# Time attention in blocks of 64 keys, one sequence per half of the rows, on 64x32 tiles

## The chip, the cores and the metric

The kernel runs on one core of a Trainium2 chip. Every array is fp32. The metric is the device time of one execution in microseconds; the lower, the better. PE is TensorE (matmuls; PEld its weight loads), DVE VectorE, ACT ScalarE, POOL GpSimd, SP the engine that issues most DMAs.

## The reference

The input x has the shape 2 x 256 x 128 x 128: batch, time T, band F, channel C. Three residual steps follow each other. Time attention runs causally over the 256 times of each of the 2 x 128 (batch, band) pairs, band attention over the 128 bands within a distance of 16, and the feed-forward step has 512 hidden channels. The change concerns the first.

```python
xt = _ln(x, ln_t_w, ln_t_b).transpose(0, 2, 1, 3)
x = x + _mha(xt, t_wi, t_bi, t_wo, t_bo, 4, causal).transpose(0, 2, 1, 3)
x = x + _mha(_ln(x, ln_f_w, ln_f_b), f_wi, f_bi, f_wo, f_bo, 4, band)
x = x + gelu(_ln(x, ln_n_w, ln_n_b) @ w1.T + b1) @ w2.T + b2

def _mha(x, wi, bi, wo, bo, h, mask):        # dh = 32
    q, k, v = split_heads(x @ wi.T + bi)
    attn = softmax(q k^T / sqrt(dh) + mask)
    return (attn @ v) @ wo.T + bo
```

## The kernel before

The work is cut into groups of 512 tokens, on which every step works with tiles of 128 partitions by 512 columns. The first 128 groups (class OverTime) are time attention; each holds two whole sequences of 256 times, s = 0 and 1. After them come 128 groups of band attention (OverBands) and 128 of feed-forward (FeedForward), in runs of 8 and 8. Nothing reorders the instructions: each engine executes in the order in which `run` writes them, a loop over n that does one part of several groups in each turn (software pipelining). The order of the matmuls of the scores is a table written by hand, TIME_ORDER.

One group of time attention goes through these steps, spread over several turns:

- statistics, root, normalize, turn, fetch: layer norm on DVE (roots of four groups at once by ACT's Ln and Exp, sharpened on DVE by `refine`), transposed by DVE and through a DRAM tile on SP's queue into xnT, channels on partitions.
- queries_keys, take_query, take_key: two products of 512 columns into PSUM banks, copied by ACT into qT and kT. `product` makes each as four matmuls on 128x32 tiles of PE (rows x columns of the array), which write 32 partitions each.
- values, take_values: four blocks of 128 tokens, tokens on partitions, into two banks (vp0, vp1), copied by ACT into v.
- scores: keys on partitions, queries on columns, by 32x64 tiles. The first 128 keys of a sequence meet all its queries (first_scores, into the four banks a0 to a3, one for each head); the second 128 keys meet only the second 128 queries (second_scores, banks b0 to b3) one turn later. Keys are taken in halves of 64, so that columns ahead of a half are skipped.
- first_weights, second_weights: ACT's Exp into p0 and p1, head by head. mask_first, mask_second: POOL zeroes what lies above the diagonal (affine select). add: POOL adds p1 to the second half of p0, for the sums.
- weigh: PE sums the weights over the keys by a product with ones (into rp) and weighs the values (into op), on 128x32 tiles.
- invert (ACT: Ln, Exp of -Ln) and divide (DVE: a Newton step, u, then oT = op times u); output (PE, into yp), finish (DVE adds the residual) and store.

A turn n does the second part of the scores of group n (`old`), the first part of n + 1 (`new`), the queries, keys and values of n + 2, weigh of n - 1 and output of n - 2. Eight PSUM banks carry the roles a0 to a3 and b0 to b3; hand_banks_on moves the roles round after every turn, and Attention.place says which step borrows which bank. A bank is free for the next writer when its last reader is done, and PE executes in order, so a matmul that waits for a bank holds up all that is behind it. A fp32 matmul shows as two records in the trace.

All instructions bear the line of a helper (L907 before, `InOrder`), so groups are told apart by the names of their tiles.

Of the kernel before, what the change touches and what calls it, by code (L numbers as in the profile page):

```python
# [33 lines left out]
HALF = P // 2  # L34
LARGE = 1e20
# [334 lines left out]
class Group:  # L370
# [50 lines left out]
    def root_in_spare(self):  # L421
        path = self.path
        self.root_by_scalar(path.ps[path.banks["b2"]][:, BANK - self.mv.shape[1] :])

    def root_in_bank(self):
        path = self.path
        self.root_by_scalar(path.ps[path.banks["b2"]][:, 0 : self.mv.shape[1]])
# [84 lines left out]
    def queries_keys(self):  # L512
        pass
# [47 lines left out]
class Attention(Group):  # L561
    which = None
    swapped = ()
# [7 lines left out]
    def queries_keys(self):  # L571
        path = self.path
        wf = path.k.wf[self.which]
        self.qp = path.bank([P, NT * P], "qp", self.place.get("qp", path.held.pop("qp", None)))
        product(path, self.qp, wf[:, 0:P], self.xnT)

        self.kp = path.bank([P, NT * P], "kp", self.place.get("kp"))
        product(path, self.kp, wf[:, P : 2 * P], self.xnT)
# [11 lines left out]
    def values(self):  # L590
        path = self.path
        wv = path.k.wf[self.which][:, 2 * P : 3 * P]
        self.vp = path.bank([P, NT, P], "vp", self.place.get("vp"))
        for i in range(NT):
            product(path, self.vp[:, i], self.xnT[:, i * P : (i + 1) * P], wv, turn=2 if i in self.swapped else 0)
# [19 lines left out]
    def divide(self):  # L615
# [10 lines left out]
        vector.scalar_tensor_tensor(u, self.rp, 2.0, self.r0, ALU.subtract, ALU.mult)  # L626
        self.oT = path.work.tile([P, NT * P], F32, name="oT", bufs=2)
        vector.tensor_tensor(by_rows(self.oT), by_tile(self.op), by_tile(u), ALU.mult)

    def output(self):  # L630
        path = self.path
        self.yp = path.bank([P, NT, P], "yp", self.place.get("yp", path.held.pop("yp", None)))
        for i in range(NT):
            product(path, self.yp[:, i], self.oT[:, i * P : (i + 1) * P], path.k.wn[self.which])
# [11 lines left out]
def product(path, out, weights, x, start=True, stop=True, turn=0):  # L646


    for c in range(P // D):
        path.tensor.matmul(out[rows_of(c)], weights[:, rows_of((c + turn) % NT)], x, start=start, stop=stop)  # L650


class OverTime(Attention):
# [4 lines left out]
    swapped = (1, 3)  # L658
    early, late = (1, 2), (0, 3)

    def values(self):
        path = self.path
        wv = path.k.wf[self.which][:, 2 * P : 3 * P]
        self.vp = [path.bank([P, 2, P], "vp", self.place.get(f"vp{s}")) for s in range(2)]
        for i in range(NT):
            product(
                path, self.vp[i // 2][:, i % 2], self.xnT[:, i * P : (i + 1) * P], wv, turn=2 if i in self.swapped else 0
            )
# [7 lines left out]
    def first_tiles(self):  # L676
        path = self.path

        self.p0 = path.work.tile([P, 2, H, 2 * P], F32, name="p0", tag="p", bufs=3)
        self.s0 = {h: path.bank([P, 2, 2 * P], "sp", path.banks[f"a{h}"]) for h in range(H)}  # L680

    def second_tiles(self):
        path = self.path

        self.p1 = path.work.tile([P, 2, H, 2, P], F32, name="p1", tag="h", bufs=2)
        self.s1 = {h: path.bank([P, 2, P], "sp", path.banks[f"b{h}"]) for h in range(H)}

    def first_scores(self, h, s, e):
        r, a = rows_of(h), 2 * s * P
        self.path.tensor.matmul(  # L690
            self.s0[h][e : e + HALF, s, e:], self.kT[r, a + e : a + e + HALF], self.qT[r, a + e : a + 2 * P],
            start=True, stop=True,
        )

    def second_scores(self, h, s, e):
        r, a, q = rows_of(h), (2 * s + 1) * P, P - HALF - e
        self.path.tensor.matmul(
            self.s1[h][e : e + HALF, s, q:], self.kT[r, a + q : a + q + HALF], self.qT[r, a + q : a + P],
            start=True, stop=True,
        )  # L700

    def first_weights(self, heads):
        for h in heads:
            self.path.scalar.activation(self.p0[:, :, h], self.s0[h], AF.Exp)

    def second_weights(self, heads):
        for h in heads:
            self.path.scalar.activation(self.p1[:, :, h, 0], self.s1[h], AF.Exp)

    def mask(self, blk, base=0):  # L710
        path = self.path
        path.gpsimd.affine_select(
            out=blk, in_=blk, compare_op=ALU.is_ge, fill=path.zero, base=base,
            pattern=[[0, 2], [0, H], [1, blk.shape[-1]]], channel_multiplier=-1,
        )

    def mask_first(self):
        self.mask(self.p0[:, :, :, 0:P])

    def mask_second(self):  # L720
        self.mask(self.p1[0:HALF, :, :, 0], -HALF)
        self.mask(self.p1[HALF:P, :, :, 0, 0:HALF])

    def add(self, s):
        self.path.gpsimd.tensor_tensor(self.p1[:, s, :, 1], self.p1[:, s, :, 0], self.p0[:, s, :, P : 2 * P], ALU.add)

    def weigh(self):
        path, v = self.path, self.v
        rp = path.bank([P, 2, 2, P], "rp", self.place.get("rp"))
        for n in range(2):  # L730
            for h in range(H):
                w = self.p1[:, :, h, 1] if n else self.p0[:, :, h, 0:P]
                path.tensor.matmul(rp[rows_of(h), :, n], path.k.ones[:, 0:D], w, start=True, stop=True)
        op = path.bank([P, 2, 2 * P], "op", self.place.get("op"))
        for s in range(2):
            for h in range(H):
                r = rows_of(h)
                path.tensor.matmul(op[r, s, :], v[:, 2 * s, r], self.p0[:, s, h], start=True, stop=False)
# [774 lines left out]
```

## Time and profile before

| | before |
|---|---|
| median of 3 runs (lowest, highest) | 2633.42 us (2632.39, 2633.75) |
| span of the profiled execution | 2631.9 us |
| PE busy, share of the span | 99% |
| DVE, ACT, POOL busy | 81%, 70%, 74% |
| DMA queue of the loads and stores, share of 16 engines | 50.5% |
| granted PE clock | 1.000 |

The page gives the profiled execution by its span, from its first to its last instruction; no other time of that execution is given. Rows of a timeline give start, length, engine and operation, out<-in by the names of the tiles, the number of instructions merged into the row, and in brackets the idle time before it and what ended it. `128*32 128x512` is a PE tile of 128 rows by 32 columns with 512 columns of moving data. Rows of groups give, behind the count, the busy time, the mean length of one in ns and the idle time before.

### The profile page before, as it was taken

Reading aid. Unit: us, or ns where it says so; the run is one execution under the profiler, and the core shown is the slowest. Engines: PE = TensorE matmul, PEld = TensorE weight load, DVE = VectorE, ACT = ScalarE, POOL = GpSimd, SP = SyncE. Lnnn points to the kernel's source line nnn. Section 1 sums busy time; section 2 is a strip of 40 time slices with the busy share of each in tenths; the row PEclk is TensorE's granted clock in tenths of the full one; section 3 lists DMA queues with packets and bytes.
Section 4 is the critical chain, followed back from the end, with each engine's and each line's share of the span. In section 5 each row is a group of like instructions: output and inputs, shape, how many; then the busy total and the mean of one; then the engine's idle time right before and its main releaser. Section 6 shows DMA issues by size and latency. Waiting matters only on the chain.

```text
span 2631.9 us, 156460 instructions
## 1 busy us (share of the span) xinstructions
PE 2617.8 (99%) x68688; PEld 1837.4 (70%) x68688; DVE 2140.8 (81%) x6410; ACT 1838.8 (70%) x3543; POOL 1958.6 (74%) x2311
## 2 busy tenths in 40 slices
PE   9999999999999999999999999999999999999999
PEld 6666666666766767666777776667676677777776
DVE  8888888888888887977878779788797797887974
ACT  7989988999899875564655746647557466475573
POOL 7999999999999987666667666665776666757762
PEclk9999999999999999999999999999999999999999
DMA  6656555565565454445454544554454445554543
GB/s 155 167 149 158 149 149 149 155 155 149 149 158 149 122 127 119 115 123 127 118 124 124 123 122 117 126 128 120 122 126 120 120 119 131 123 120 123 123 104 88
DMA packets 469797, 344.97 MB, mean 131 GB/s; under 512 B 43120, under 2 KB 404464, under 8 KB 469104
## 3 DMA queue, kind: packets, MB, share of 16 engines
q1 hardware_dynamic: 468408, 334.41, 50.5%
q8 instruction: 540, 8.85, 1.5%
q14 instruction: 153, 1.25, 0.2%
q10 hardware_dynamic: 696, 0.46, 0.1%
HBM read 167.98 MB, written 166.72 MB: 127 GB/s over the span
## 4 chain that ended last, share of the span: by engine, by line
PE 99%; DVE 0%; issue 0%; DMA 0%; ACT 0%; ACTq 0%; DVEq 0%
PE bank L907 99%; DMA x<-in_x 0%; DVE xh L907 0%; DVE bank L907 0%; DVE res L907 0%; DVE stats L907 0%; DVE oT L907 0%; DVE u L907 0%; DVE xnT L907 0%; ACTq L907 0%; ACT p L907 0%; DVE vy L907 0%; ACT lnv L907 0%; DVE mv L907 0%; ACT root L907 0%
## 5 line engine op out<-in xcount | busy, mean ns | idle before, releaser
L907 ACT ACTIVATE hT<-bank,b 128x512 f32<-128x512 f32 x512 | 348.1, 688 | 524.2 <-PE bank L907 483.2
L907 POOL TENSOR_SCALAR_AFFINE_SELECT pf<-pf 128x512 f32<-128x512 f32 x768 | 477.7, 637 | 185.3 <-ACT pf L907 159.1
L907 PEld LDWEIGHTS bank<-w2T_sb,hT 128*32 128x32 f32 x16384 | 467.4, 110 | 54.8 <-issue 29.0
L907 PE MATMUL bank<-xnT,wf 128*32 128x512 f32 x4096 | 492.4, 592 | 0.5 <-DVE xnT L907 0.5
L907 PE MATMUL bank<-xnT,w1f 128*32 128x512 f32 x4096 | 486.3, 592 | 0.2 <-issue 0.2
L907 PE MATMUL bank<-w2T_sb,hT 128*32 128x128 f32 x16384 | 482.8, 273 | 1.0 <-issue 1.0
L907 ACT ACTIVATE p<-bank 128x512 f32<-128x512 f32 (+1 forms) x1024 | 430.6, 494 | 62.9 <-PE bank L907 62.9
L907 DVE TENSOR_SCALAR xh<-x,mv,rstd 128x160 f32<-128x160 f32 (+1 forms) x1012 | 394.3, 432 | 59.7 <-POOL rstd L907 49.4
L907 POOL TENSOR_SCALAR_AFFINE_SELECT p<-p 128x1024 f32<-128x1024 f32 (+2 forms) x384 | 364.5, 949 | 57.5 <-ACT p L907 49.1
L907 PEld LDWEIGHTS bank<-wf,xnT 128*32 128x32 f32 x8192 | 243.3, 110 | 144.1 <-issue 101.6
L907 POOL TENSOR_TENSOR p<-p,p 128x512 f32<-128x512 f32 x256 | 324.6, 1291 | 10.6
L907 DVE BATCH_NORM_STATS2 stats<-x 128x6 f32<-128x128 f32 x1536 | 329.0, 276 | 3.4 <-DMA x<-in_x 3.4
L907 POOL TENSOR_SCALAR rstd<-mv 128x4 f32<-128x4 f32 x251 | 57.8, 230 | 361.7 <-DVE mv L907 360.5
L907 PEld LDWEIGHTS bank<-xnT,w1f 128*32 128x32 f32 x4096 | 183.6, 110 | 171.6 <-issue 109.6
L907 PE MATMUL bank<-qT,kT 32*64 32x80 f32 (+4 forms) x16384 | 302.0, 271 | 0.1
L907 PEld LDWEIGHTS bank<-qT,kT 32*64 32x64 f32 x16384 | 260.0, 131 | 51.2 <-ACT kT L907 50.6
L907 DVE TENSOR_TENSOR res<-bank,res 128x512 f32<-128x512 f32 (+1 forms) x259 | 170.3, 658 | 153.3 <-PE bank L907 144.7
L907 ACT ACTIVATE pf<-bank 128x512 f32<-128x512 f32 x512 | 265.8, 602 | 35.5 <-PE bank L907 31.3
L907 PE MATMUL bank<-wn,oT 128*32 128x128 f32 x8192 | 283.8, 274 | 0.1
L907 DVE STREAM_TRANSPOSE z<-xh 128x512 f32<-128x512 f32 x380 | 270.3, 711 | 13.3
L907 PE MATMUL bank<-wf,xnT 128*32 128x128 f32 x8192 | 276.5, 273 | 0.0
L907 POOL TENSOR_TENSOR rstd<-rstd,mhalf 128x4 f32<-128x4 f32 x251 | 260.8, 1039 | 20.9
(100 smaller groups left out, 3820.3 us busy)
## 6 DMA issues: line engine op xcount, KB each, us to landing
turned<-z SPq DMA_DIRECT2D x1520, 64.0 KB, 2.7
xnT<-turned SPq DMA_DIRECT2D x380, 256.0 KB, 3.2
x<-res SPq DMA_DIRECT2D x256, 128.0 KB, 2.5
x<-x SPq DMA_DIRECT2D x128, 256.0 KB, 4.1
out<-res SPq DMA_DIRECT2D x252, 128.0 KB, 2.3
x<-in_x SPq DMA_DIRECT2D x124, 256.0 KB, 4.3
x<-in_x SPq DMA_DIRECT2D x4, 128.0 KB, 2.8
x<-in_x SPq DMA_DIRECT2D x6, 64.0 KB, 2.9
```

The source lines that it names most:

```text
L907: return self.tc.keep_in_program_order(emit(*args, **kwargs))
```

## The change

Each of the two sequences of a group now keeps to one half of the partitions, from the values on. Keys go in four blocks b of 64, of which each meets the queries from its own first one on: 256, 192, 128 and 64 columns.

- Values are written by 128x64 tiles, a block of sequence 0 into partitions 0 to 63 and of sequence 1 into 64 to 127.
- Scores keep their 32x64 tiles and their columns. A bank of heads a0 to a3 now holds blocks 0 and 1 (448 of 512 columns), b0 to b3 blocks 2 and 3 (192 columns); the partition half is the sequence.
- Exponentials cover 448 and 192 columns for 512 and 256. Masks are four affine selects of 64 partitions by 512; POOL adds 512, 256 and again 256 columns for the sums.
- Sums and weighted values run on 64x32 tiles: eight matmuls at a time, four heads by two sequences. [...]
- Queries, keys and output of time attention use 128x64 tiles for 128x32.
- The bank roles no longer move; places are fixed (yp in b3, queries and keys in b0, vp0 in a3, vp1 in a0). The roots go into a0, and refine runs within divide.
- The queries of n + 2 move between the scores and weigh; keys, output and values stay behind weigh. The order of Exp changes with it (heads 0, 1, 2 of b, heads 1, 2 of a; late: head 3 of b, heads 3, 0 of a).

On PE, one turn before, from the end of the scores to the start of the next (bank and pair numbers are PSUM banks; wf with xnT are queries and keys where the column count is 512 and values where it is 128; wn with oT is the output):

```order
L907 MATMUL bank_115<-qT,kT 64x64
L907 MATMUL bank_113<-wn_236,oT 32x128 x16
L907 MATMUL bank_112<-p_5261,ones 32x2x128 x4
L907 MATMUL bank_112<-p_5428,ones 32x2x128 x4
L907 MATMUL bank_110<-p_5261,v 32x256 x4
L907 MATMUL bank_110<-p_5428,v 32x128 x4
L907 MATMUL bank_110<-p_5261,v 32x256 x4
L907 MATMUL bank_110<-p_5428,v 32x128 x4
L907 MATMUL bank_109<-xnT,wf_151 32x512 x4
L907 MATMUL bank_111<-xnT,wf_151 32x512 x4
L907 MATMUL bank_113<-wf_151,xnT 32x128 x8
L907 MATMUL bank_115<-wf_151,xnT 32x128 x8
```

and after (pair_123 is b1 and b2, pair_124 a1 and a2, bank_116 b0, bank_117 b3, bank_118 a0, bank_119 a3):

```order
L925 MATMUL bank_117<-qT,kT 64x64 x2
L925 MATMUL bank_116<-xnT,wf_152 64x512 x2
L925 MATMUL pair_123<-p_5657,ones 32x128 x8
L925 MATMUL pair_123<-p_5838,ones 32x128 x8
L925 MATMUL pair_123<-p_5657,ones 32x128 x8
L925 MATMUL pair_124<-p_5657,v 32x256 x8
L925 MATMUL pair_124<-p_5657,v 32x192 x8
L925 MATMUL pair_124<-p_5838,v 32x128 x8
L925 MATMUL pair_124<-p_5838,v 32x64 x8
L925 MATMUL bank_116<-xnT,wf_152 64x512 x2
L925 MATMUL bank_117<-wn_225,oT 64x128 x8
```

The output moved behind the keys, the queries stand alone ahead of the sums, and the instructions of sums and weighted values went from 24 to 56.

Where a turn ends on PE, after: the last rows are the values, then the first scores of the next turn:

```order
L925 MATMUL bank_119<-wf_152,xnT 64x128 x4
L925 MATMUL bank_118<-wf_152,xnT 64x128 x4
L925 MATMUL bank_119<-qT,kT 64x256 x2
L925 MATMUL bank_116<-qT,kT 64x128 x2
L925 MATMUL pair_123<-qT,kT 64x128 x4
```

The values' two banks are again written by the scores: bank_119 by the very next matmul, which waits for ACT's copy of it (v<-bank_119). Before, the first scores wrote other banks than the values did.

On ACT, one turn after, from the copy of the keys on (before, ln and r stood between the six first Exp and the last two, and the query's copy right ahead of the key's):

```order
L925 COPY kT<-bank_116 128x512
L925 COPY v<-bank_119 128x256
L925 COPY v<-bank_118 128x256
L925 ACTIVATE p_8585<-bank_116 128x192
L925 ACTIVATE p_8585<-pair_123 128x192 x2
L925 ACTIVATE p_8584<-pair_124 128x448 x2
L925 ACTIVATE qT<-bank_116,bq_188 128x512
L925 ACTIVATE ln<-pair_123 128x512
L925 ACTIVATE r_8700<-ln 128x512
L925 ACTIVATE p_8585<-bank_117 128x192
L925 ACTIVATE p_8584<-bank_119 128x448
L925 ACTIVATE p_8584<-bank_118 128x448
```

The diff, cut to its core:

```diff
+FIRST = 4 * P - HALF
+SECOND = P + HALF
...
-def product(path, out, weights, x, start=True, stop=True, turn=0):
-    for c in range(P // D):
-        path.tensor.matmul(out[rows_of(c)], weights[:, rows_of((c + turn) % NT)], x, start=start, stop=stop)
+def product(path, out, weights, x, columns=D, start=True, stop=True):
+    for c in range(0, P, columns):
+        path.tensor.matmul(out[c : c + columns], weights[:, c : c + columns], x, start=start, stop=stop)
...
+        for b in range(NT):
+            for s in range(2):
+                a = 2 * s * P + b * HALF
+                path.tensor.matmul(
+                    self.vp[b // 2][half(s), b % 2], self.xnT[:, a : a + HALF], wv, start=True, stop=True
+                )
...
+    def block(self, b):
+        return (0, 2 * P, 0, P)[b], 2 * P - b * HALF
+    def scores(self, b, h, s):
+        sp, r = (self.s1 if b // 2 else self.s0)[h], rows_of(h)
+        a, n = self.block(b)
+        t = 2 * s * P + b * HALF
         self.path.tensor.matmul(
+            sp[half(s), a : a + n], self.kT[r, t : t + HALF], self.qT[r, t : t + n], start=True, stop=True
         )
...
+    def mask(self, p, n):
+        for s in range(2):
+            blk = p[half(s)].rearrange("p h (b q) -> p (h b) q", q=n)[:, :, 0:HALF]
...
+    def add(self):
+        add = self.path.gpsimd.tensor_tensor
+        late = self.folded[:, :, HALF:P]
+        add(self.folded, self.p0[:, :, P : 2 * P], self.p1[:, :, 0:P], ALU.add)
+        add(self.spare, self.p0[:, :, FIRST - HALF : FIRST], self.p1[:, :, P:SECOND], ALU.add)
+        add(late, late, self.spare, ALU.add)
...
+        self.rp, self.op = path.wide
+        tiles = [(h, s) for s in range(2) for h in range(H)]
+        for p, a, at in ((self.p0, 0, 0), (self.folded, 0, P), (self.p0, 2 * P, HALF)):
+            for h, s in tiles:
+                q = 2 * s * P + at
                 path.tensor.matmul(
+                    self.rp[rows_of(h), q : q + P], path.k.ones[half(s), 0:D], p[half(s), h, a : a + P],
+                    start=at == 0, stop=at == HALF,
                 )
...
 TIME_ORDER = """
-    s310 s301 s011 s000 s300 s010 s001 f110 f201 f200 f111 f301 f101 f310 f000 f211
+    030 031 200 201 210 211 220 221 300 301 310 311 320 321 010 011 020 021
...
-        self.banks = dict(zip(("a1", "a2", "b0", "b3", "a0", "a3", "b1", "b2"), range(8)))
+        self.banks = dict(zip(("b0", "b3", "b1", "b2", "a1", "a2", "a0", "a3"), range(8)))
...
-                Attention.place = dict(yp=b["b0"], rp=b["b3"], op=b["a1"], qp=b["a2"], kp=b["b1"], vp0=b["b0"], vp1=b["b2"])
+                Attention.place = dict(yp=b["b3"], qp=b["b0"], kp=b["b0"], vp0=b["a3"], vp1=b["a0"])
...
+            if old is not None and n + 2 >= TURNED:
+                do_at(n + 2, OverTime, "queries", "take_query")
...
             do(n - 1, "weigh")
...
+            if old is not None:
+                old.second_weights((3,))
+                old.mask_second()
+                old.add()
             if new is not None:
                 new.first_weights(new.late)
+            roots = sets[n // 2] if n in (3, 5) else fours.get(n + 2 * NT)
+            if roots is not None:
+                roots.root_in_spare("a0")
...
+                do_at(n + 2, OverTime, "keys", "take_key")
+                do(n - 2, "output")
+            if roots is not None:
+                groups[n - 1].divide(roots.refine)
+            else:
+                do(n - 1, "divide")
```

In TIME_ORDER a row of three digits is block, head, sequence.

More of the change, by code (lines that the diff above doesn't have):

```diff
@@ L510, in second_mask, with queries, keys @@
         pass
-    def queries_keys(self):
+    def queries(self):
+        pass
+    def keys(self):
         pass
@@ L562 @@
     which = None
-    swapped = ()
+    columns = D
     place = {}
@@ L569, in bias, with queries, keys @@
         )
-    def queries_keys(self):
+    def queries(self):
         path = self.path
-        wf = path.k.wf[self.which]
         self.qp = path.bank([P, NT * P], "qp", self.place.get("qp", path.held.pop("qp", None)))
-        product(path, self.qp, wf[:, 0:P], self.xnT)
+        product(path, self.qp, path.k.wf[self.which][:, 0:P], self.xnT, self.columns)
+    def keys(self):
+        path = self.path
         self.kp = path.bank([P, NT * P], "kp", self.place.get("kp"))
-        product(path, self.kp, wf[:, P : 2 * P], self.xnT)
+        product(path, self.kp, path.k.wf[self.which][:, P : 2 * P], self.xnT, self.columns)
     def take_query(self):
@@ L633, in output @@
         for i in range(NT):
-            product(path, self.yp[:, i], self.oT[:, i * P : (i + 1) * P], path.k.wn[self.which])
+            product(path, self.yp[:, i], self.oT[:, i * P : (i + 1) * P], path.k.wn[self.which], self.columns)
     def finish(self):
@@ L663, in values @@
         wv = path.k.wf[self.which][:, 2 * P : 3 * P]
[L664 to L668, printed above, removed]
+        self.vp = [path.bank([P, 2, P], "vp", self.place.get(f"vp{i}")) for i in range(2)]
+        for b in range(NT):
[4 more added lines that the diff above has]
+                )
     def take_values(self):
@@ L748 @@
+        for b in range(NT):
+            p = (self.p0, self.p1)[b // 2]
+            a, n = self.block(b)
+            for h, s in tiles:
+                r, q = rows_of(h), 2 * s * P + b * HALF
+                path.tensor.matmul(
+                    self.op[r, q : q + n], v[half(s), b, r], p[half(s), h, a : a + n], start=b == 0, stop=b == NT - 1
+                )
 TIME_ORDER = """
-    s310 s301 s011 s000 s300 s010 s001 f110 f201 f200 f111 f301 f101 f310 f000 f211
-    f210 f100 f001 s111 f010 s311 s201 f300 f311 s211 f011 s100 s210 s101 s110 s200
+    030 031 200 201 210 211 220 221 300 301 310 311 320 321 010 011 020 021
@@ L751 @@
+    000 001 130 131 110 111 120 121 100 101 230 231 330 331
 """.split()
@@ L760, in time_scores @@
         old.second_tiles()
-    for kind, h, s, e in TIME_ORDER:
-        if kind == "s" and old is not None:
-            old.second_scores(int(h), int(s), int(e) * HALF)
-        if kind == "f" and new is not None:
-            new.first_scores(int(h), int(s), int(e) * HALF)
+    for order in TIME_ORDER:
+        b, h, s = map(int, order)
+        group = old if b // 2 else new
+        if group is not None:
+            group.scores(b, h, s)
 class OverBands(Attention):
@@ L941, in __init__, with single_banks, split_pairs @@
             )
+    def single_banks(self, ctx, name, banks):
+        pool = ctx.enter_context(self.tc.tile_pool(name=name, bufs=1, space=PSUM))
+        for i in banks:
+            self.ps[i] = pool.tile([P, BANK], F32, name=f"bank{i}", tag=f"bank{i}")
+    def split_pairs(self):
+        self.pairs.close()
+        self.single_banks(self.pairs, "rest", range(2, 6))
+        self.rotation = [0, 1, 6, 7, 2, 3, 4, 5]
+        self.next_bank = 0
     def turn_of_bank(self):
-        i, self.next_bank = self.next_bank, (self.next_bank + 1) % 8
+        i = self.rotation[self.next_bank]
+        self.next_bank = (self.next_bank + 1) % len(self.rotation)
         return i
@@ L1227, in start @@
         self.fold_value(0)
-        Attention.place = dict(qp=2, kp=3, vp0=6, vp1=7)
-        first.queries_keys()
+        Attention.place = dict(qp=b["b0"], kp=b["b3"], vp0=b["b1"], vp1=b["b2"])
+        first.queries()
+        first.keys()
         first.take_query()
@@ L1258, in start @@
         first.mask_first()
-        second.queries_keys()
+        second.queries()
+        second.keys()
         second.take_query()
```

166 lines of the change are left out of this document (66 added, 100 removed).

## The prediction

> **What bounds the kernel now.** I read the page first, then busy time by stage, then the timeline of one group in the middle of the time stage, and last the groups of each engine there.
>
> ```profile
> span 2631.9 us, 156460 instructions
> PE 2617.8 (99%) x68688; PEld 1837.4 (70%) x68688; DVE 2140.8 (81%) x6410; ACT 1838.8 (70%) x3543; POOL 1958.6 (74%) x2311
> PE 99%; DVE 0%; issue 0%; DMA 0%; ACT 0%; ACTq 0%; DVEq 0%
> ...
> 24.00:914.00 890.00, 888.17 (x24056) 616.38 (x24048) 755.89 (x2257) 800.47 (x1821) 822.70 (x753) 1.00 0.59 151
> 914.00:2632.00 1718.00, 1708.68 (x44354) 1207.15 (x44354) 1368.05 (x4069) 1024.75 (x1694) 1122.93 (x1535) 1.00 0.48 120
> ```
>
> TensorE (PE) is the bound: it is busy all the span at the full clock and carries the chain that ended last. The change touches the time stage, some 900 us. There POOL is busy 92% and ACT 90%, so they have little room. One group on PE:
>
> ```profile
> 500.68 1.06 PE L907 MATMUL bank<-wf,xnT 128*32 128x128 f32 x32
> 501.67 1.39 PE L907 MATMUL bank<-qT,kT 32*64 32x64 f32 x64
> 502.98 1.08 PE L907 MATMUL bank<-wn,oT 128*32 128x128 f32 x32
> 503.88 1.05 PE L907 MATMUL bank<-p,ones 128*32 128x256 f32 x16
> 504.74 1.48 PE L907 MATMUL bank<-p,v 128*32 128x256 f32 x32
> 506.04 1.90 PE L907 MATMUL bank<-xnT,wf 128*32 128x512 f32 x16
> 507.76 0.95 PE L907 MATMUL bank<-wf,xnT 128*32 128x128 f32 x28
> ...
> 1101.05 3.62 PE L907 MATMUL bank<-xnT,w1f 128*32 128x512 f32 x32
> 1104.48 3.68 PE L907 MATMUL bank<-w2T_sb,hT 128*32 128x128 f32 x128
> 1107.98 3.62 PE L907 MATMUL bank<-xnT,w1f 128*32 128x512 f32 x32
> ```
>
> From start to start a group lasts 507.76 - 500.68 = 7.08 us. An fp32 product shows twice in the trace, so it is two passes. Four tiles run side by side: 32 records of 512 columns are eight passes in 3.43 us, 0.429 each; 128 records of 128 columns are 32 passes in 3.50, 0.109 each; sums, four passes of 256 columns, take 0.86, 0.215 each. The group then reads: values 0.99 (eight passes are 0.87, and 0.11 more before the tile shape changes), scores 1.31 (1.20 and 0.11 for the change back), output 0.90, sums 0.86, weighted values 1.30 (four passes of 256 columns and four of 128), queries and keys 1.72. Each change of tile shape costs about 0.11 us, and there are two per group.
>
> **The change, part by part.** *Sums and weighted values on 64x32 tiles.* Eight tiles instead of four, with keys in blocks of 64. Sums go from four passes of 256 columns to three products of 128, six passes: 6 x 0.109 = 0.65, against 0.86. Weighted values go to passes of 256, 192, 128 and 64 columns, two each: 2 x (0.215 + 0.162 + 0.109 + 0.055) = 1.08, plus 0.03 because eight tiles start staggered, against 1.30. This saves 0.40 if eight tiles of this shape run side by side. No row has 64x32; the nearest has eight tiles too:
>
> ```profile
> 958.18 0.97 PE L907 MATMUL bank<-qT,kT 32*64 32x80 f32 x64
> ...
> L907 PE MATMUL bank<-qT,kT 32*64 32x80 f32 x8192 | 124.0, 240 | 0.1
> ...
> 960.84 1.06 PE L907 MATMUL bank<-wn,oT 128*32 128x128 f32 x32
> ...
> 13.08 1.16 PE L907 MATMUL bank<-ident,xh 128*128 128x128 f32 x8
> ...
> L907 PE MATMUL bank<-wf,xnT 128*32 128x128 f32 x8192 | 276.5, 273 | 0.0
> ```
>
> Those 64 records start within 0.97 less the 0.24 that one lasts, 11.6 ns apart; 13.6 are needed for passes of 128 columns on eight tiles. So I take the full gain; the other end is that pairs of row tiles take turns, which would make both phases twice as long (+1.73 us a group).
> [...]
>
> *128x64 tiles for queries, keys, values and output.* Half as many instructions, equal columns. 128x128 tiles run 128 columns in (1.16 - 0.27 - 0.11)/7 = 0.11 too (0.27 for the last record, 0.11 for the first weight load), so a pass costs the same on either side of 64, and I take no gain. Only the first weight load after a change of shape is exposed: 1.08 against 1.06 for 32 columns (the output with and without a change ahead), 0.11 for 128; 0.05 for 64.
>
> *Queries between scores and sums.* PE now changes shape four times a group (the pieces of order on PE, above): scores to queries, queries to sums, weighted values to keys, values to scores: two more changes, 2 x 0.11, and loads of 0.05 + 0.02 + 0.05 where 0.02 stood. PE alone: scores 1.20, change 0.16, queries 0.86, change 0.13, sums 0.65, weighted values 1.11, change 0.16, keys 0.86, output 0.87, values 0.87, change 0.11: 6.98 us, only 0.10 less than now.
>
> *A wait that the order of banks adds.* The scores that come first write bank a3, and the values that come just before them went into a3 and a0 (vp0, vp1). Before, the banks first written by the scores were free long ago. Now PE stands, with all scores queued behind the first, until ACT has copied vp0:
>
> ```profile
> 500.93 0.59 ACT L907 COPY kT<-bank 128x512 f32<-128x512 f32 x1
> 501.41 0.76 ACT L907 COPY v<-bank 128x256 f32<-128x256 f32 x2
> ...
> 508.01 0.59 ACT L907 COPY kT<-bank 128x512 f32<-128x512 f32 x1 [0.17 <-PE bank L907]
> ...
> 14.35 0.69 DVE L907 COPY xnT<-bank 128x512 f32<-128x512 f32 x1 [1.70 <-PE bank L907]
> 15.09 1.06 PE L907 MATMUL bank<-xnT,wf 128*32 128x512 f32 x8 [0.51 <-DVE xnT L907]
> ...
> L907 ACT COPY v<-bank 128x256 f32<-128x256 f32 x226 | 84.8, 375 | 1.4
> ```
>
> From the end of the keys (507.76, the next start) to ACT is 0.25 us; a copy of 256 columns takes 0.375; from the end of a copy to PE is 15.09 - 15.04 = 0.05. So the next scores start 0.44 (half of the values) + 0.25 + 0.375 + 0.05 = 1.12 after the values start, where PE would be ready at 0.98. The group becomes 6.00 + 1.12 = 7.12. vp1's copy reaches PE at 0.87 + 0.25 + 0.375 + 0.05 = 1.55, 0.43 after the scores start, and a0 is wanted once its tiles have done 192 columns of head 0, at 0.05 + 0.32 = 0.37. The 1.20 of the scores already holds idle time of tiles (640 columns in two passes are 1.07), so I count 0.02 of these 0.06.
>
> *The roots, in every fourth group.* They are now written into a0 and refined on DVE inside divide, between u and oT. The values that go into a0 wait for that:
>
> ```profile
> 497.73 0.34 ACT L907 ACTIVATE lnv<-mvs,eps 128x16 f32<-128x16 f32 x1
> ...
> 498.73 0.17 DVE L907 SCALAR_TENSOR_TENSOR rstds<-vy,bank 128x16 f32<-128x16 f32 x1
> ...
> 505.62 0.63 ACT L907 ACTIVATE r<-ln 128x512 f32<-128x512 f32 x1
> 506.16 1.07 ACT L907 ACTIVATE p<-bank 128x512 f32<-128x512 f32 x2
> ```
>
> Counted from the scores' start, sums end at 3.00, ln starts at 3.25, r 0.63 later, the three late exponentials 0.54 after that and then 0.21, 0.42 and 0.42 apart, so lnv starts at 5.5 and rstds ends 1.17 later, near 6.7; PE wants a0 at 6.44. That is about 0.27 lost there and, as vp1's copy is late too, some 0.05 at the scores: 0.32 in four groups, 0.08 a group. Together 7.22.
>
> *What is hidden.* ACT does 448 and 192 columns for 512 and 256:
>
> ```profile
> L907 ACT ACTIVATE p<-bank 128x512 f32<-128x512 f32 x450 | 257.0, 596 | 0.0
> L907 ACT ACTIVATE p<-bank 128x256 f32<-128x256 f32 x450 | 161.6, 390 | 55.0 <-PE bank L907 55.0
> ...
> L907 POOL TENSOR_TENSOR p<-p,p 128x512 f32<-128x512 f32 x226 | 286.7, 1291 | 9.4
> L907 POOL TENSOR_TENSOR res<-x,orow 128x512 f32<-128x512 f32 x113 | 144.8, 1281 | 0.0
> L907 POOL TENSOR_SCALAR_AFFINE_SELECT p<-p 128x1024 f32<-128x1024 f32 x113 | 124.5, 1101 | 0.0
> L907 POOL TENSOR_SCALAR_AFFINE_SELECT p<-p 64x1024 f32<-64x1024 f32 x113 | 122.9, 1088 | 43.9 <-ACT p L907 43.9
> L907 POOL TENSOR_SCALAR_AFFINE_SELECT p<-p 64x512 f32<-64x512 f32 x113 | 74.5, 659 | 7.4
> ```
>
> (596 - 390)/256 = 0.8 ns a column, 64 columns in each of eight, 0.41 us less; PE hides it, and ACT has 13% or more of the group idle. POOL has four masks of 64x512 (4 x 0.66) for 1.10 + 1.09 + 0.66, and adds of 512, 256 and 256 for two of 512. A 256 add lies between 0.65 (half) and 1.29 (no saving); I take 0.75, nearer to half, since the masks fall from 1.09 to 0.66 when halved. Sum 2.64 + 1.29 + 1.50 + 1.28 = 6.7, some 6.8 with its waits, under 7.22. DVE does the same work; u and oT end before the scores want their banks. The queries need xnT 3.8 us earlier in the group, and finish's stores now stand ahead of the fetch on SP; the fetch is issued a whole group ahead and lands in 3.2 us:
>
> ```profile
> xnT<-turned SPq DMA_DIRECT2D x380, 256.0 KB, 3.2
> ```
>
> so about 3 us of cover stay. If that went, the queries would stop PE, and the sums behind them. Start, transition and the bands and feed-forward stages keep their work; I take 0, within 2 us either way.
>
> **Sum.** 7.22 - 7.08 = 0.14 us, times 890/7.08 = 126 groups: 18 us slower. The profiled span is 2631.9, 1.5 under the median of 2633.4; the median becomes 2651.
>
> **Rivals.** (1) *Faster: PE's own work decides*, neither ACT's copy nor the roots make it wait. The group is 6.98, 13 us less: 2621; and down to 6.90 (2610) if the scores pack as their columns allow, 1.07 and 0.05 for the first load, since the new order starts all eight tiles at once. For it: now PE runs locked to its own sum, 7.08. Against: the copy's 1.12 comes from rows. It decides once the copy answers within 0.98. (2) *Even:* the copy waits, but the scores pack and the roots cost half: 7.22 - 0.08 - 0.04 = 7.10, between 7.04 and 7.12: 2628 to 2638. (3) *POOL becomes the bound:* if a 256 add costs like a 512 one, POOL needs 7.8 us, +0.7, and 2633 + 88 = 2721; it decides where such an add exceeds about 0.95. The masks' slope speaks against it. [...]
>
> **How the numbers follow.** Forecast (2640 to 2668) 0.54, faster 0.22, even 0.15, POOL 0.06, issue or turns 0.03. A measurement can tell about 0.2%, 5.3 us, from no change: slower 0.54 + 0.06 + 0.03 = 0.63, same 0.15, faster 0.22. The range reaches to 2620, rival 1 without the better packing, and to 2672, where changes of shape cost 0.15 instead of 0.11; it leaves out the deep end of rival 1 and rivals 3 and 4, under 0.2 together.
>
> **What would show it.** Starts of the scores 7.2 us apart in the time stage, with PE's loads idle on ACT's v ahead of them; sums near 0.65 and weighted values near 1.1 long, four gaps of about 0.1; every fourth group longer by 0.3, on DVE's rstds; POOL under 95%. It would be wrong if the scores start within 1.0 of the values, if a wait for POOL's adds stands before the sums, or if the eight tiles take longer than 1.8 for both phases.

## The result, and the profile after

The changed kernel takes 2717.72 us (median of 4 runs, 2711.37 to 2720.73) against 2633.59 (2632.39 to 2635.34) for the kernel before on the same chip: ratio 1.0314, 95% interval 1.0299 to 1.0329, slower by 3.1%. The sign was forecast; the size was not: 18 us forecast, 84 measured. The profiled execution has a span of 2716.4 us.

The page of the changed kernel:

```profile
span 2716.4 us, 162951 instructions
PE 2677.5 (99%) x71760; PEld 1946.7 (72%) x71760; DVE 2142.0 (79%) x6410; ACT 1802.4 (66%) x3543; POOL 1947.7 (72%) x2567
PE 95%; ACT 3%; DVE 1%; issue 1%; DMA 0%; SPq 0%; ACTq 0%; DVEq 0%
```

The time stage and the rest, by windows (length, then busy time and count of PE, PEld, DVE, ACT and POOL, PE clock, DMA share, GB/s):

```profile
24.00:990.00 966.00, 943.52 (x27004) 683.59 (x27006) 755.38 (x2247) 763.82 (x1818) 811.02 (x1001) 1.00 0.55 140
990.00:2716.00 1726.00, 1713.97 (x44558) 1250.27 (x44554) 1370.61 (x4080) 1026.15 (x1697) 1123.99 (x1542) 1.00 0.48 120
```

PE still carries the chain, at the full clock, but in the time stage it is now idle for 22 us of 966 where it was idle for 2 of 890. POOL is busy 811 of 966 us, 84%. One undisturbed turn on PE (timeline; the scores run from 503.13 to 504.73):

```profile
503.13 0.43 PE L925 MATMUL bank<-qT,kT 32*64 32x256 f32 x4
...
504.73 1.08 PE L925 MATMUL bank<-xnT,wf 128*64 128x512 f32 x4
505.74 0.94 PE L925 MATMUL pair<-p,ones 64*32 64x128 f32 x48
506.42 1.34 PE L925 MATMUL pair<-p,v 64*32 64x256 f32 x64
507.69 1.08 PE L925 MATMUL bank<-xnT,wf 128*64 128x512 f32 x4
508.60 1.04 PE L925 MATMUL bank<-wn,oT 128*64 128x128 f32 x16
509.48 1.04 PE L925 MATMUL bank<-wf,xnT 128*64 128x128 f32 x16
510.56 0.43 PE L925 MATMUL bank<-qT,kT 32*64 32x256 f32 x4
```

From start to start: scores 1.60, queries 1.01, sums 0.68, weighted values 1.27, keys 0.91, output 0.88, values 1.08: 7.43 us, against 7.08 before and 7.14 forecast (7.22 with the share of the roots). Where the 84 us are, counted from the starts of the scores of all turns:

| | us |
|---|---|
| undisturbed turns, (7.43 - 7.08) x 124 | 43 |
| roots, 0.28 more in every fourth turn | 9 |
| turns that last longer than that, at irregular places: 26 us in all against 3 us before | 23 |
| up to the first regular turn | 3 |
| from the last turn to the end | 6 |

The forecast missed 66 of the 84 us. The scores make 30 of them: 1.60 us where the forecast has 1.36 with the change of shape, 0.24 in each of 124 turns. That term and the irregular turns are most of what the prediction lacked.

**The scores.** The same windows over one phase of scores, after and then before (read the count of PEld, the weight loads):

```profile
503.12:503.60 0.48, 0.47 (x31) 0.47 (x34) 0.48 (x3) 0.37 (x1) 0.48 (x2) 1.00 0.06 17
503.60:503.79 0.19, 0.19 (x20) 0.11 (x6) 0.19 (x3) 0.00 (x0) 0.19 (x1) 1.00 0.00 0
503.79:504.70 0.91, 0.91 (x36) 0.80 (x30) 0.91 (x8) 0.69 (x3) 0.83 (x2) 1.00 0.42 101
```

```profile
501.66:502.12 0.46, 0.46 (x32) 0.46 (x34) 0.46 (x4) 0.45 (x2) 0.46 (x2) 1.00 0.84 207
502.12:502.31 0.19, 0.19 (x23) 0.19 (x13) 0.19 (x2) 0.06 (x1) 0.19 (x1) 1.00 0.93 210
502.31:502.95 0.64, 0.64 (x44) 0.58 (x28) 0.64 (x6) 0.38 (x1) 0.64 (x1) 1.00 0.96 283
```

A window counts what overlaps it. After, 34 + 30 are all 64 loads of the 32 scores: none starts between 503.60 and 503.79. The 34 are the two passes of 17 scores; the 18th score's first load starts 0.67 us after the first score's, and from there new scores come 16.7 ns apart. Before, loads start all through the middle window; by the starts of the records, 22 scores are under way before a pause of 0.11 us, which ends at 0.72.

**The irregular turns.** One of them, in the timeline, and PE's own waits from 100 to 900 us, after and before:

```profile
475.15 1.28 PE L925 MATMUL pair<-p,v 64*32 64x256 f32 x57
477.31 0.31 PE L925 MATMUL pair<-p,v 64*32 64x64 f32 x7 [0.88 <-issue]
```

```profile
PE pair L925 <- issue: 7.2, 11, 1.4
```

```profile
PE bank L907 <- issue: 1.3, 1, 1.3
```

PE stops in the middle of the weighted values, seven matmul records before their end, and no semaphore ends the wait ("issue"). The DMA view has a queue for instructions (q8), whose packets have 16 KB:

```profile
q8 instruction: 564, 9.24, 1.5%
```

That is 564 packets for PE's 71760 matmul records, one for 127; before there are 540 for 68688, one for 127 too. A fp32 matmul has two records, so by these counts a packet holds the instructions of 64 matmuls, with as many weight loads (PEld x71760) 254 records in all. In the example the last packet before the stop starts at 474.6 and the matmuls resume 2.7 us later; at ten of the long stops that distance is 2.3 to 2.9 us.

Not all of the 26 us are of this kind. The longest irregular turn stands near the start, takes 4.5 us more than the others, and begins with a wait for data:

```profile
46.62 1.98 PE L925 MATMUL bank<-xnT,wf 128*64 128x512 f32 x4 [2.66 <-DMA xnT<-turned]
```

These are the queries, which the change moved ahead of the sums: the prediction named this wait and counted on about 3 us of cover. So some 21 us are left for stops of the first kind.

### The profile page after: what moved, and what is told of

Same layout as the page of the kernel before. It is cut to its first block, busy times and chain, and to the rows that moved or that the text cites. A ratio compares the mean times of both kernels' runs of the same rounds, so it can differ in the third digit from the quotient of the medians.

```text
span 2716.4 us, 162951 instructions
## 1 busy us (share of the span) xinstructions
PE 2677.5 (99%) x71760; PEld 1946.7 (72%) x71760; DVE 2142.0 (79%) x6410; ACT 1802.4 (66%) x3543; POOL 1947.7 (72%) x2567
## 4 chain that ended last, share of the span: by engine, by line
PE 95%; ACT 3%; DVE 1%; issue 1%; DMA 0%; SPq 0%; ACTq 0%; DVEq 0%
PE bank L925 82%; PE pair L925 13%; ACT p L925 1%; ACT r L925 1%; ACT ln L925 1%; DVE vy L925 0%; DMA xnT<-turned 0%; ACT lnv L925 0%; ACT bank L925 0%; DVE rstds L925 0%; DVE stats L925 0%; DVE xh L925 0%; DMA x<-in_x 0%; SPq L925 0%; DVE res L925 0%
## 5 line engine op out<-in xcount | busy, mean ns | idle before, releaser
L925 PE MATMUL bank<-xnT,wf 128*32 128x512 f32 (+1 forms) x3068 | 525.4, 601 | 5.6 <-DMA xnT<-turned 2.7
L925 PE MATMUL bank<-xnT,w1f 128*32 128x512 f32 x4096 | 500.6, 592 | 0.0
L925 POOL TENSOR_SCALAR_AFFINE_SELECT p<-p 64x512 f32<-64x512 f32 x512 | 334.9, 654 | 137.1 <-ACT p L925 122.6
L925 PE MATMUL bank<-qT,kT 32*64 32x80 f32 (+4 forms) x12288 | 335.0, 262 | 5.8 <-DVE res L925 0.8
L925 PEld LDWEIGHTS bank<-xnT,w1f 128*32 128x32 f32 x4096 | 212.5, 110 | 152.0 <-issue 80.3
L925 PEld LDWEIGHTS bank<-wn,oT 128*32 128x32 f32 (+1 forms) x6144 | 245.9, 119 | 85.2 <-ACT p L925 44.5
L925 PEld LDWEIGHTS bank<-wf,xnT 128*32 128x32 f32 (+1 forms) x6120 | 242.7, 119 | 78.8 <-issue 63.6
L925 PE MATMUL bank<-wn,oT 128*32 128x128 f32 (+1 forms) x6144 | 284.7, 273 | 3.3 <-issue 1.9
L925 PE MATMUL bank<-wf,xnT 128*32 128x128 f32 (+1 forms) x6120 | 280.2, 273 | 4.2 <-DVE rstds L925 3.9
L925 POOL TENSOR_TENSOR p<-p,p 128x512 f32<-128x512 f32 (+1 forms) x256 | 251.2, 1002 | 10.6
```

Source lines behind the costliest of these rows:

```text
L925: return self.tc.keep_in_program_order(emit(*args, **kwargs))
```

## The experiments

The experiments test theory A: PE lacks instructions, in two ways: within the scores (17 stand ready, the rest comes late) and at the ends of blocks of 64 matmuls, which come no faster than a fetch allows. Its rivals are the waits for ACT's copies of v (theory B), and the tiles, banks and table themselves. Ratios are against the kernel before.

### The table of the scores in another order

```
-    030 031 200 201 210 211 220 221 300 301 310 311 320 321 010 011 020 021
-    000 001 130 131 110 111 120 121 100 101 230 231 330 331
+    030 031 200 201 210 211 220 221 010 011 020 021 300 301 000 001 130 131
+    310 311 320 321 110 111 120 121 100 101 230 231 330 331
```

> The changed kernel, with the table of the scores reordered: after the first eight entries come the blocks 0 of heads 1, 2 and 0 and block 1 of head 3, so that each of the eight tiles holds 256 columns and more within the first 18 entries; the blocks 3 of heads 1 and 2 go behind them. Same matmuls, same waits. In the changed kernel each turn's 18th score starts 0.67 us after the first, while the 17th starts at 0.37, and from there they come 16.7 ns apart. Theory A (instruction supply): about 17 matmuls stand ready when the scores start, the next arrive 0.65 us later whatever they are, so it counts how many columns the first 17 hold. Then the scores fall from 1.60 to about 1.30 us, the turn from 7.43 to 7.13, times 124 turns: 37 us, about 2680 us. Theory B (the wait of head 0's block 0 for ACT's second copy of v holds up the stream): that wait now stands at the 15th entry, the gap comes ahead of it, and the scores keep 1.6 us or more: 2715 us or more. Theory C (eight tiles cannot pack these columns better): no change, 2717.

2720.17 us, ratio 1.0313 (1.0288 to 1.0338): no gain, where theory A had 2680. The scores did fall, but to 1.47 and not to 1.30, and the undisturbed turn to 7.29; the 18th score again came 0.67 after the first. In the profiled execution, the slowest of four, the mean turn is 7.73 against 7.66: the irregular turns grew from 19 to 44 us (turns 8 to 123), more than the 17 us that the scores gave. PE's waits from 100 to 900 us:

```profile
PE pair L925 <- issue: 11.9, 12, 2.4
PE bank L925 <- issue: 6.5, 12, 1.0
```

So the two ways seem to hang together: what the scores save is used up at the next end of a block. The second order moves only the scores that wait for ACT's second copy:

```
-    000 001 130 131 110 111 120 121 100 101 230 231 330 331
+    130 131 110 111 120 121 000 001 100 101 230 231 330 331
```

> The changed kernel, with head 0's block 0 (the scores that wait for ACT's second copy of v) moved from the 19th and 20th place of the table to the 25th and 26th, behind head 3's block 1 and heads 1 and 2's blocks 1. Theory A (instruction supply): the gap stays behind the 17th score (start of the 18th at 0.67 us after the first), the scores last 1.60 us or more, since tile row 0 gets its 448 columns later: 2715 to 2735 us. Theory B (that wait holds up the stream): the gap moves to just ahead of the 25th or is gone, 1.35 to 1.45 us, 2690 us.

2725.67 us. The gap stayed behind the 17th score, at 0.67, and the scores grew to 1.70: within theory A's range, against B.

### The roots elsewhere, and the values ahead of the output

```
-                roots.root_in_spare("a0")
+                roots.root_by_scalar()
```

> The changed kernel, with the roots of four groups written by ACT to SBUF instead of PSUM bank a0, so that the values need not wait for DVE's refine. The values of every fourth turn lasted 1.37 us where the others took 1.08. Theory (the wait for the bank costs 0.29 us in 30 turns): every turn's values near 1.08, 9 us less, 2709 us. Rival (DVE or ACT late in that turn moves the wait elsewhere, to the copy of v or the output): under 3 us less.

2753.77 us, ratio 1.0455 (1.0438 to 1.0473): about 35 us slower than the changed kernel, where 9 us less were expected. The values did come down to 1.08 in every turn, but in every fourth turn the next scores rose from 1.60 to 2.88, waiting for oT: the rival's direction, far beyond its size. PE's wait and groups of DVE in this run (100 to 900 us), a timeline of DVE and POOL, and last two rows of the changed kernel:

```profile
PE pair L925 <- DVE oT L925: 26.6, 24, 1.2
...
L925 DVE SCALAR_TENSOR_TENSOR vy<-vy,root 128x16 f32<-128x16 f32 x25 | 31.4, 1255 | 0.9
L925 DVE SCALAR_TENSOR_TENSOR rstds<-vy,root 128x16 f32<-128x16 f32 x25 | 16.2, 646 | 0.9
```

```profile
496.99 0.17 DVE L925 SCALAR_TENSOR_TENSOR vy<-mvs,root 128x16 f32<-128x16 f32 x1
...
497.16 1.95 POOL L925 TENSOR_TENSOR p<-p,p 128x512 f32<-128x512 f32 x2
...
497.20 1.26 DVE L925 SCALAR_TENSOR_TENSOR vy<-vy,root 128x16 f32<-128x16 f32 x1
```

```profile
517.15 1.96 POOL L925 TENSOR_TENSOR p<-p,p 128x512 f32<-128x512 f32 x2
517.16 0.17 DVE L925 SCALAR_TENSOR_TENSOR vy<-vy,bank 128x16 f32<-128x16 f32 x1
```

With both inputs in SBUF, an instruction on 16 columns lasts 1.26 us while POOL adds (1255 ns on the mean of 25). With the root in PSUM it takes 0.17 beside the same add (171 ns on the mean of 26 in the changed kernel), and here another one takes 0.17 ahead of the add. Why the place of the root counts is not shown.

> The changed kernel with the roots in SBUF, and the values moved ahead of the output (keys, values, output), so that both copies of v are done before the scores start. Theory A (the gap in the scores is instruction supply, and the copies cost only the 0.13 us ahead of the first score): from the last product to the scores 0.98 us instead of 1.08, the scores keep their gap and 1.60 us, perhaps with a wait for finish at head 3's second blocks; 2717 - 9 (roots) - 12 = 2696 us. Theory B (the copies' waits make the gap): the scores fall to 1.36 us too, 2666 us.

The edit beside that of the roots: `do_at(n + 2, OverTime, "keys", "take_key", "values", "take_values")` ahead of the output, and the values' old place only where no scores follow. 2744.48 us, with the roots' loss in it; theory A had 2696, with a gain from the roots. From the last product to the scores it is 0.97 instead of 1.08, so the wait for the copy cost 0.11; the gap and the 1.60 of the scores stayed, outside the turns of the roots. The keys took 0.09 more instead (1.00), and the undisturbed turn is 7.47; as an estimate from the changed kernel, where the Exp that reads the values' bank a3 ends 0.96 us after the keys start, the values wait for it. Theory B is out for the gap: here both copies end ahead of the scores.

```
-                roots.root_in_spare("a0")
+                roots.root_in_spare("b1")      # 16 columns behind the 192 of the scores
```

> The changed kernel, with the roots of four groups in 16 columns of PSUM bank b1 that nobody else uses, instead of a0 (or of SBUF, where DVE's refine took 2.08 us beside POOL instead of 0.51). The values then wait for no refine, and refine keeps its 0.5 us. Theory: the values last 1.08 us in every turn, 0.29 us less in 30 turns, 9 us: 2709 us. Rival (the time saved turns into stalls for instructions, as in the run with the reordered table): 2715 to 2720 us with every value phase at 1.08.

2743.82 us, ratio 1.0406 (1.0388 to 1.0425). The values were 1.08 in every turn and refine kept 0.17 us an instruction, but now DVE's first step of divide came after ACT's write into the same pair of banks (b1 and b2, which hold the sums), and the scores waited again, 2.61 us in every fourth turn:

```profile
489.77 0.70 DVE L926 TENSOR_TENSOR pair<-pair,r 128x512 f32<-128x512 f32 x1 [2.73 <-ACT pair L926]
```

Both attempts lose 1.0 to 1.3 us in four turns where they save 0.28. The place in a0 costs 0.28 us in four turns, the least of the three.

### More and fewer matmuls

The width of the tiles of queries, keys and output is one line, `columns = HALF`; it was set to 128, to 32, and to 32 with the values in pieces of 32 tokens too. In the last of these, H1 is that long matmuls ahead of the scores make the gap, H2 that it belongs to the scores:

```
-    columns = HALF
+    columns = P        # the first;  D in the second and third
```

> The changed kernel, with queries, keys and output on 128x128 tiles instead of 128x64: the same columns and waits in 6 matmuls instead of 12, 102 instead of 108 in a turn. Theory (PE's instructions come in blocks, one fetch for 64 matmuls, and a turn that uses them up too fast stands until the next block is in): undisturbed turn within 0.1 us of 7.43 (first weight loads 0.06 longer each), stalls from 25 us in the time stage to about 12: 2705 to 2715 us. Rival (the stalls come from waits or memory traffic, not from the number of instructions): stalls stay at 25, 2717 to 2729 us.

> The changed kernel, with queries, keys and output on 128x32 tiles as in the kernel before: 120 matmuls in a turn instead of 108, the same columns and waits. My prediction put the width of these tiles at no cost either way. Theory (instruction supply): undisturbed turn about 7.43 us (less 0.05 for shorter first weight loads), stalls in the time stage from 25 to 60 us or more: 2745 us or more. Rival (stalls independent of the number of instructions): 2710 to 2717 us.

> The changed kernel with all products of time attention on 128x32 tiles, the values too: ahead of the scores PE then runs 16 short matmuls, as in the kernel before, instead of 8 long ones; 128 matmuls in a turn. The 18th score started 0.67 us after the first in every kernel with 8 values matmuls (or 8 output matmuls) ahead of the scores, whatever the order of the table. Theory H1 (the supply of instructions runs on only as fast as the work ahead takes them, so 8 long matmuls leave it idle and it is late for the scores): the gap behind the 17th score goes, the scores fall from 1.60 to about 1.4 us; the whole is slower all the same, since the number of matmuls brings more stalls at the block ends: 2780 us or more. Rival H2 (the gap belongs to the scores' own order, tiles or waits): the scores keep 1.60 us and the gap.

Then the sums without their third product, the kernel before with its sums and weighted values cut up, and the kernel before with nothing but its values on 128x64 tiles:

```
-        for p, a, at in ((self.p0, 0, 0), (self.folded, 0, P), (self.p0, 2 * P, HALF)):
+        for p, a, at in ((self.p0, 0, 0), (self.folded, 0, P)):
```

> The changed kernel without the third product of the sums (keys of the second block of 64, for queries 64 to 191 of a sequence), which leaves the sums incomplete: 100 matmuls in a turn instead of 108, in the densest stretch. Six passes of 128 columns become four: the sums fall from 0.68 to 0.46 us, 27 us less. Theory (stalls follow the number of matmuls): the stalls of the time stage fall too, from 25 to about 12 us: 2678 us. Rival (they do not): 2690 us.

```
-                path.tensor.matmul(rp[rows_of(h), :, n], path.k.ones[:, 0:D], w, start=True, stop=True)
+                for s in range(2):
+                    path.tensor.matmul(rp[rows_of(h), s, n], path.k.ones[:, 0:D], w[:, s], start=True, stop=True)
...                  # op: 128 columns, then twice 64 + 64, for 256 and 128
```

> The kernel before, with the matmuls of its sums and weighted values cut into pieces of 128 and 64 columns: 56 matmuls instead of 24 on the same 128x32 tiles, the same columns, no other change; 128 matmuls in a turn instead of 96. Theory (instruction supply): the phases of an undisturbed turn keep their lengths (7.08 us), but the time stage gets stalls that it did not have (3 us): 60 us or more, since a block of 64 matmuls would have to last 3.5 us where the changed kernel averages 4.5; 2690 to 2860 us. Rival (the stalls of the changed kernel come from its 64x32 tiles, its banks or its waits): 2634 to 2640 us.

> The kernel before, with its values on 128x64 tiles (8 matmuls for 16), nothing else changed: one more change of tile shape, keys to values, some 0.15 us a turn. Theory H1: the scores that follow now show a gap behind the 17th and grow from 1.32 to 1.45 us or more; 7.08 + 0.15 + 0.15 = 7.38, 2670 us. Rival H2: the scores stay at 1.32, the turn at 7.23, 2652 us.

Measured, by the number of matmuls in a turn. The mean turn and the undisturbed one are from the starts of the scores (the undisturbed one without the turns of the roots); us a block is the mean distance of the instruction packets in the time stage; idle is PE's wait on "issue" from 100 to 900 us. The kernel before took 2633.6 to 2638.4 us beside these runs.

| kernel | matmuls | undisturbed | mean turn | us a block | idle | time |
|---|---|---|---|---|---|---|
| before, values on 128x64 | 88 | 7.23 | 7.26 | 5.23 | 1.1 | 2656.93 |
| before | 96 | 7.08 | 7.10 | 4.69 | 1.3 | 2633.59 |
| after, two products of sums | 100 | 7.21 | 7.34 | 4.67 | 3.1 | 2676.95 |
| after, tiles of 128 | 102 | 7.69 | 7.84 | 4.88 | 2.9 | 2736.77 |
| after | 108 | 7.43 | 7.66 | 4.52 | 7.5 | 2717.72 |
| after, tiles of 32 | 120 | 7.55 | 8.27 | 4.38 | 34.2 | 2788.31 |
| after, all of 32 | 128 | 7.42 | 8.39 | 4.18 | 52.4 | 2804.13 |
| before, sums and values cut up | 128 | 7.25 at the least | 8.27 | 4.12 | 62.7 | 2790.77 |

The last row is the plainest: the kernel before, with the same columns on the same tiles, banks and waits, loses 152 us against the kernel before beside it (2638.4; ratio 1.0576, 1.0555 to 1.0597) through 32 more matmuls in a turn. Two of its turns, and its waits:

```profile
478.89 1.07 PE L916 MATMUL bank<-p,ones 128*32 128x128 f32 x27
481.78 0.30 PE L916 MATMUL bank<-p,ones 128*32 128x128 f32 x2 [1.82 <-issue]
...
488.52 1.07 PE L916 MATMUL bank<-p,ones 128*32 128x128 f32 x26
491.00 0.30 PE L916 MATMUL bank<-p,ones 128*32 128x128 f32 x2 [1.41 <-issue]
```

```profile
PE bank L916 <- issue: 62.7, 76, 1.8
```

The stop is at nearly the same place in both turns, since 128 matmuls are two blocks. So the irregular turns need neither the new tiles nor the new banks. In all traces no two packets of the time stage are less than 3.3 us apart, so a stretch of 64 matmuls that PE would do faster can end in a stop. That 3.3 us is what a fetch needs is an inference: it is the least distance seen. Over a whole turn it would be no limit (108 matmuls are 1.7 blocks, 5.6 us at that distance), but after, scores to weighted values are 90 matmuls in 4.6 us, and the 18 of keys, output and values take 2.9. Before, the 72 from scores to weighted values took 4.4.

Fewer matmuls by wider tiles don't pay: 2736.77 us, where 2705 to 2715 were expected. Waits on "issue" fell from 7.5 to 2.9 us, but on 128x128 tiles queries and keys grew by 0.05 each, output and values by 0.11 and 0.05. The last two are one more change of shape, since the values stay on 128x64: on tiles of 32, where the output differs from the values too, both grow by the same amounts, and with all tiles of 32 by 0.00 and 0.03. Removing eight matmuls and a quarter of a us from the sums gave 41 us, of which 27 are columns and 12 fewer stops (19 to 7 us, turns 8 to 123): the theory's number. And 128x64 values in the kernel before cost 0.15 a turn, one change of shape, and left its scores at 1.32: together with the run on all tiles of 32, where 16 short matmuls stand ahead of the scores and the gap remained, that refutes H1. The gap belongs to the scores.

### Loads twice

`dma_start` of each x in the time stage written twice:

> The changed kernel, with each load of x in the time stage issued twice (the same data to the same place), 256 KB more in every turn. Theory (the stalls are instruction fetches that share the DMA engines with the data): fetches take longer than their median of 1.19 us, stalls in the time stage grow from 25 to 40 us or more, the undisturbed turn stays at 7.43: 2730 us or more. Rival (the stalls have nothing to do with the DMA engines): 2717 us.

2985.31 us, ratio 1.1328 (1.1286 to 1.1371), but for another reason: the queries waited for the fetch of xnT behind the loads.

```profile
PE bank L925 <- DMA xnT<-turned: 132.5, 60, 3.9
```

The mean turn of 9.8 us leaves 5.8 us for 64 matmuls, and waits on "issue" are 2.8 us from 100 to 900 us. The instruction packets of the time stage took 1.20 us at the median, as without the loads (1.19). So nothing shows that the data slow the fetches; as a test of the stops the run fails.

### What the 18th score waits for

The last two reorder the table once more: short pieces first (300 to 321 ahead of 200 to 221), and large ones first, as shown. P1 is that the 18th score comes at a fixed time, P2 that its time follows the first scores:

```
+    030 031 200 201 010 011 020 021 300 301 130 131 210 211 220 221 000 001
+    310 311 320 321 110 111 120 121 100 101 230 231 330 331
```

> The changed kernel; in the table of the scores the pieces of 64 columns (block 3, heads 0 to 2) change places with the pieces of 128 (block 2), so the same 17 scores come first, but the ninth and later ones find their tiles free at 0.11 us instead of 0.18. P1 (17 matmuls stand ready, the next come 0.67 us after the first whatever runs): the 18th at 0.67, the scores 1.60 us, 2717 us. P2 (the supply starts again when the first eight have left, about 0.5 us after the ninth is taken): the 18th at 0.60, the scores 1.53, 2709 us.

> The changed kernel; the table starts with the largest pieces that may start (head 3's and heads 1 and 2's blocks 0), so that the first 17 hold 3072 columns instead of 2432, and the ninth score finds its tile free only at 0.2 us or later. P1 (the next come at 0.67 whatever runs): the 18th at 0.67, the scores 1.45 to 1.50 us. P2 (0.5 us after the ninth is taken): the 18th at 0.72 or later. By the fetches (blocks of 64 matmuls come no faster than one in 3.4 us, in every run so far), the whole gains less than the scores do, if anything: 2710 to 2725 us.

2724.13 and 2725.19 us. With short pieces first, the ninth score's load starts at 0.12 instead of 0.18, and yet the gap ends at the same 0.67 and the scores last 1.60. With large ones first the first load behind the gap starts at 0.674 too, and the scores last 1.57. P2 falls: the time is the same in all five tables of the changed kernel, whatever the first scores do. P1 had that right, but not the length of the scores with large pieces first, 1.45 to 1.50. What fixes the time, whether it is a lack of instructions at all, and why 22 scores stand ready in the kernel before and 17 after, stays open. No version tried here beats the kernel before: the best order of the scores saves 17 us and pays them at the blocks, and no other term measured here is near 84 us.

## Why the prediction was wrong in size

- *Scores.* The step that failed: "The 1.20 of the scores already holds idle time of tiles", a length taken over from the old table, and 0.16 for the change. Measured 1.60 for 1.36. The new table gives head 0 only 192 columns for each sequence, and one tile of head 2 as few, among the first 17 scores; those tiles stand until the rest comes at 0.67. In the old table 22 scores are under way by then. This is 30 us of the missing 66. That the order counts is shown (1.47 to 1.70 us by the table alone); what holds back the 18th score is not.
- *Instructions as a resource* had no term at all. Sums and weighted values on eight tiles were counted by columns, and their 56 matmuls for 24 at no price. The 0.03 for "issue or turns" among the chances stands for a price of each matmul or for tiles that take turns, and no run shows either: the 48 records of the sums start 14 ns apart on the mean, and the two phases take 1.95 us, where turns would make them 3.46 (2 x 1.73). In the runs above the time goes with the blocks of 64: 32 more matmuls in a turn of the kernel before raise PE's waits on "issue" from 1.3 to 62.7 us. In the changed kernel this is about 18 us: the irregular turns have 26, less 3 before and less the 4.5 of the early turn.
- *Sums and weighted values*: 0.65 and 1.11 + 0.16 forecast, 0.68 and 1.27 measured. By these lengths eight 64x32 tiles do run side by side. Right.
- *The wait for the copy of vp0*: 1.12 forecast from the values to the scores, 1.08 measured, and the wait itself is there:

```profile
510.13 0.81 ACT L925 COPY v<-bank 128x256 f32<-128x256 f32 x2 [0.57 <-PE bank L925]
510.55 0.15 PEld L925 LDWEIGHTS bank<-qT,kT 32*64 32x64 f32 x4 [0.28 <-ACT v L925]
```

  Moving the values took it away (0.97). vp1's copy, 0.02, cost nothing that can be seen: it ends 0.38 us after the scores start, and the 19th score wants it later than the gap ends (0.67).
- *The roots*: 0.32 in every fourth turn forecast, 0.28 measured, on the row named:

```profile
517.68 0.66 PE L925 MATMUL bank<-wf,xnT 128*64 128x128 f32 x8 [0.17 <-DVE rstds L925]
```

- *Changes of shape*: 0.13 to 0.16 forecast with the first weight load; the kernel before with one more pays 0.15, the changed one on tiles of 128 or 32 pays 0.16. Right. *128x64 tiles at no cost*: queries 1.01 for 0.99, keys 0.91 for 0.86, output 0.88 for 0.87; right within 0.05.
- *POOL*: an add of 256 columns was taken as 0.75 us and masks of 64x512 as 0.66. Groups of POOL from 100 to 900 us:

```profile
L925 POOL TENSOR_SCALAR_AFFINE_SELECT p<-p 64x512 f32<-64x512 f32 x417 | 272.7, 654 | 104.1 <-ACT p L925 92.2
L925 POOL TENSOR_TENSOR p<-p 128x256 f32<-128x256 f32 x105 | 76.4, 728 | 8.2
L925 POOL TENSOR_TENSOR p<-p,p 128x256 f32<-128x256 f32 x105 | 76.4, 727 | 0.0
```

  0.73 and 0.65; rival 3 did not come, although its 2721 is near the time measured: the right number for the wrong reason. Rivals 1 and 2 fell with the scores, whose 1.60 neither of them allows.
- *The fetch of xnT* was counted as hidden, with about 3 us of cover. It was, but for the early turn, where PE waits 2.7 us for it. With the loads doubled the cover is gone in most turns.
- *Start, transition and later stages at 0, within 2 us*: 9 us, 3 up to the first regular turn and 6 behind the last. No run was made for these, and their cause is open. With the early turn's 4.5 and about 5 us from small misses in the other phases of a turn, this makes up the 66.

None of the three signs of being wrong that the prediction names came: the scores start 1.08 after the values, PE waits for no add of POOL ahead of the sums, and both phases on eight tiles last 1.8 without the change of shape. None of them looks at the scores' own length or at the number of instructions, where the loss was.

## What to carry to other kernels

Count PE's instructions as well as its columns. Where small tiles pack many matmuls into one stretch, compare the stretch with the least distance seen between its instruction packets (here 3.3 us for 64 fp32 matmuls, and 4.1 to 4.5 us on the mean of the time stage where stops are frequent), and look for waits on "issue" without a releaser. When a table of matmuls is rewritten, don't take the old phase's length over: see what each tile holds among the first ones to start (17 here, 22 in the old table). And a phase that gets shorter may pay nothing while the count of instructions stays: here 17 us less in the scores went with 25 us more of irregular turns.

## What was unexpected

- Instruction packets of 16 KB, one for 64 fp32 matmuls, in the time stage never less than 3.3 us apart; some 21 us of stops with 108 matmuls in a turn of 7.4 us, 3 us with 96 in 7.1.
- After the change of shape to the scores, 17 matmuls start at once or as soon as their tiles are free, the 18th at 0.67 us in all five orders, and then at first one in 16.7 ns. In the kernel before it is 22.
- A DVE instruction of 16 columns takes 1.26 us instead of 0.17 when both inputs lie in SBUF and POOL adds at that time; with one input in PSUM it takes 0.17 beside POOL's add too.
